# Reciprocal square roots by GpSimd's power in place of ScalarE's square root and VectorE's reciprocal

## The chip, the cores and the metric

The kernel runs on one core of a Trainium2 chip, in one launch. A core has five engines that run at the same time and wait for each other by semaphores: TensorE (PE in the profile; its weight loads are PEld), VectorE (DVE), ScalarE (ACT), GpSimd (POOL) and SyncE (SP, which only issues DMAs here). The metric is the device time of one execution, in microseconds (us). The time before is the median of three executions.

## The reference

The reference is a transformer of four blocks with three layers each: a cross-attention to a long context, a mixer over the tokens themselves, and a feed-forward layer. `x` is 2 x 128 x 256 (batch, tokens, width), the context 2 x 2048 x 256, all in float32. Every layer is `x = x + layer(_layernorm(x))`. What matters here is where reciprocal square roots stand in it:

```python
def _layernorm(x, axis=-1, eps=1e-05):
    m = jnp.mean(x, axis=axis, keepdims=True)
    v = jnp.var(x, axis=axis, keepdims=True)
    return (x - m) / jnp.sqrt(v + eps)

# block 1, feed-forward (soft mixture of experts)
def _l2norm(v, axis):
    n = jnp.sqrt(jnp.sum(v * v, axis=axis, keepdims=True))
    return v / jnp.maximum(n, L2_EPS)          # L2_EPS = 1e-12; of the tokens, and of the slots mu

# block 3, cross-attention: 16 query heads, 4 key heads of 128
def _rms_norm(x, w):
    v = jnp.mean(jnp.square(x.astype(jnp.float32)), axis=-1, keepdims=True)
    return (w * (x.astype(jnp.float32) * jax.lax.rsqrt(v + EPS))).astype(x.dtype)

# block 3, mixer (a state-space layer): 64 heads, state of N = 128
def rmsnorm(x, w):
    return x * jax.lax.rsqrt(jnp.mean(x * x, axis=-1, keepdims=True) + EPS) * w
Bm = rmsnorm((x @ WB.T).reshape(B_, L, H, N), Bn_w) + B_bias
Cm = rmsnorm((x @ WC.T).reshape(B_, L, H, N), Cn_w) + C_bias
Bm = rope(Bm, theta_cumsum)
Cm = rope(Cm, theta_cumsum)
```

In block 0 the mixer's output has a gated RMS norm too. In block 3 the cross-attention normalises and rotates 2048 + 128 keys for each of the 4 key heads and the 16 query heads; the mixer's state update is computed as products of `Cm` and `Bm` between all pairs of tokens, weighted by decays.

## The kernel before, in words

Tokens lie on the 128 partitions: `x` is one tile of 128 x 2 x 256. The layers run one after another; DMAs of weights and work that hangs only on the context (keys, values, slots) are put ahead of their layer, into gaps. A scheduler places the instructions of each engine by their dependencies and priorities, except where a helper, `InOrder` (L227 in the profile, for whatever is recorded through it), keeps those of an engine in the order of the program. In the last cross-attention's main loop and in the last mixer, TensorE, VectorE and ScalarE are kept in order in this way, GpSimd is not. SBUF and PSUM buffers come from pools, and a writer waits for the last reader of the buffer.

**Norms.** `rstd` (L148) makes the reciprocal square root of a column: ScalarE's `Sqrt` with the epsilon as bias, then VectorE's `reciprocal`. `norm_rows` (L153) is a layer norm of 128 rows: `bn_stats` and `bn_aggr` give mean and variance (tile `mv`), `rstd` the factor (tile `rs`, 128 x 1), and a `tensor_scalar` the normalised rows `xn`. Most layers call it for the two batches at their start. ScalarE evaluates its functions from tables, of which it holds one set at a time; changing from `Exp` or `Sin` to `Sqrt` puts an instruction `ACT_TABLE_LOAD` into its queue, wherever its order says so. The slots' norms (class `Slots`) use a square root on ScalarE of their own.

**The last cross-attention (L3_xattn).** Eight groups, one for each key head and batch, each with 17 tiles of keys and 4 of queries (128 x 128 each). `projected` makes them by TensorE, `squared` squares them on ScalarE, `summed` reduces on VectorE to `rs` (128 x 21, in a part of 8 and one of 13 columns), `rooted` takes the square root on ScalarE, and `rotated` starts with VectorE's reciprocal and multiplies `kq` by `rs`, then by the weights, and rotates. `turn` transposes the result. While one group is prepared, the scores, the softmax (`Exp` on ScalarE into `S`), the transposes of `S` (copied by ScalarE to `pT`) and the product with the values (`py`) of the group before are worked off. The parts of the two groups alternate in an order written by hand.

**The last mixer (L3_attn).** 16 rounds: 8 groups of 8 heads, for both batches. The rounds are pipelined: in loop pass `n` the kernel works on parts of rounds `n + 1` (angles) down to `n - 3` (gate). In a pass, for its own round, TensorE projects `pb` (`projected`; Bm and Cm of 8 heads, 128 x 1024 each), ScalarE squares them into `bc`, VectorE reduces (`squares`) to `rs` (128 x 16), and `rooted` and `scaled` follow. `scaled` is VectorE's reciprocal and 16 multiplications by ScalarE, `bc<-pb,rs`. VectorE's `decay_inputs` (`lm<-tri_incl,la`) and the last step of the angles (`sc<-mm,sc`) stand behind it. In the next pass `biased` multiplies `bc` by the norm's weights and adds the biases, `rotated` turns it into `ro`, and `turned` transposes it into `rT` by TensorE with copies by ScalarE. Then `products` and `decayed` (VectorE's `m<-mm,ex`, and GpSimd's `affine_select` of it), and `mixed` on TensorE (`mm<-m,xb`). `inputs` are GpSimd's two multiplications `xb<-xp,u` and `xb<-xp,cs`, into one buffer for each batch, which they may write when the `mixed` that read it two rounds before has ended. Since the norm's `Sqrt` and the angles' `Sin` are in different table sets, an activation of one column, `warm`, calls `Sqrt` ahead of the copies of `turned`, so that its table is loaded there:

```python
            if now:
                act.activation(warm, g.eps6, AF.Sqrt)
            if rot and n - 1 < last:
                rot.turned()
            if now:
                now.squares(0)
                now.squares(1)
                now.rooted()
            ...
            if now:
                now.scaled(halves if n == last else (slice(0, HG),))
            if nxt:
                nxt.decay_inputs()
            ...
            if mix and n - 2 < last:
                mix.mixed()
```

Of the kernel before, what the change touches and what calls it, by code (L numbers as in the profile page):

```python
# [12 lines left out]
F32 = mybir.dt.float32  # L13
# [4 lines left out]
AF = mybir.ActivationFunctionType  # L18
ALU = mybir.AluOpType
# [3 lines left out]
P = 128  # L23
B = 2
D = 256
# [10 lines left out]
class Net:  # L36


    def __init__(self, ctx, tc, ins):
        self.tc = tc  # L40
        self.nc = nc = tc.nc
        self.ins = ins
        self.n_copy = 0
        self.const = ctx.enter_context(tc.tile_pool(name="const", bufs=1, reuse_waits="tile"))
        self.small = ctx.enter_context(tc.tile_pool(name="small", bufs=2, reuse_waits="tile"))
        self.act = ctx.enter_context(tc.tile_pool(name="act", bufs=1, reuse_waits="tile"))

        c = self.const
        self.x = c.tile([P, B, D], F32, name="x")
        for b in range(B):  # L50
            nc.scalar.dma_start(self.x[:, b, :], ins["x"][b])

        self.ident = c.tile([P, P], F32, name="ident")
        make_identity(nc, self.ident)
        self.identb = c.tile([P, P], BF16, name="identb")
        make_identity(nc, self.identb)
        self.ones = c.tile([P, P], F32, name="ones")
        nc.vector.memset(self.ones, 1.0)

        self.tri_incl = c.tile([P, P], F32, name="tri_incl")  # L60
        nc.gpsimd.affine_select(out=self.tri_incl, in_=self.ones, pattern=[[1, P]],
                                compare_op=ALU.is_ge, fill=0.0, base=0, channel_multiplier=-1)

        self.tri_lt = c.tile([P, P], F32, name="tri_lt")
        nc.gpsimd.affine_select(out=self.tri_lt, in_=self.ones, pattern=[[1, P]],
                                compare_op=ALU.is_ge, fill=0.0, base=-1, channel_multiplier=-1)
        self.tri_gt = c.tile([P, P], F32, name="tri_gt")
        nc.gpsimd.affine_select(out=self.tri_gt, in_=self.ones, pattern=[[-1, P]],
                                compare_op=ALU.is_ge, fill=0.0, base=-1, channel_multiplier=1)

        self.causal = c.tile([P, P], F32, name="causal")
        nc.vector.memset(self.causal, 0.0)
        nc.gpsimd.affine_select(out=self.causal, in_=self.causal, pattern=[[-1, P]],
                                compare_op=ALU.is_ge, fill=-1e30, base=0, channel_multiplier=1)

        self.bd16 = c.tile([P, P], F32, name="bd16")
        self.blocks(self.bd16.rearrange("p (k j) -> p k j", j=16), self.ones.rearrange("p (k j) -> p k j", j=16), P // 16)
        self.iota16 = c.tile([P, 16], F32, name="iota16")
        iota_i = c.tile([P, 16], I32, name="iota_i")
        nc.gpsimd.iota(iota_i, pattern=[[1, 16]], base=0, channel_multiplier=0)  # L80
        nc.vector.tensor_copy(self.iota16, iota_i)
        self.eps5 = c.tile([P, 1], F32, name="eps5")
        nc.vector.memset(self.eps5, 1e-5)
        self.eps6 = c.tile([P, 1], F32, name="eps6")
        nc.vector.memset(self.eps6, 1e-6)
        self.half_pi = c.tile([P, 1], F32, name="half_pi")
        nc.vector.memset(self.half_pi, math.pi / 2)

# [56 lines left out]
        else:  # L145
            self.nc.vector.tensor_copy(out, in_)

    def rstd(self, out, in_, scale, eps, act=None):  # L148
        nc = self.nc
        (act or nc.scalar).activation(out, in_, AF.Sqrt, bias=eps, scale=scale)  # L150
        nc.vector.reciprocal(out, out)

    def norm_rows(self, out, in_, act=None):  # L153

        nc = self.nc
        st = self.sm([P, 6], "st")
        nc.vector.bn_stats(st, in_)
        mv = self.sm([P, 2], "mv")
        nc.vector.bn_aggr(mv, st)
        rs = self.sm([P, 1], "rs")  # L160
        self.rstd(rs, mv[:, 1:2], 1.0, self.eps5, act)
        nc.vector.tensor_scalar(out, in_, mv[:, 0:1], rs, ALU.subtract, ALU.mult)

    def layernorm(self):
# [185 lines left out]
class Values:  # L350


    KVH, HD = 4, 128
# [344 lines left out]
def l0_attn(g):  # L698

    nc, tc = g.nc, g.tc  # L700
# [4 lines left out]
    with tc.tile_pool(name="l0a", bufs=2, reuse_waits="tile") as p:  # L705
# [6 lines left out]
        act = InOrder(tc, nc.scalar)  # L712
# [26 lines left out]
        for b in range(B):  # L739
            tok = slice(b * P, (b + 1) * P)  # L740
            pss = g.mm([P, 1])
            g.project(pss, lambda c: osq[:, c, tok], lambda c: g.ones[:, 0:1])
            rs = g.sm([P, 1], "rs")
            g.rstd(rs, pss, 1.0 / D, g.eps5)
            po = g.mm([P, D])
            g.project(po, lambda c: yT[:, c, tok], lambda c: wo[:, c, :])
            nc.vector.scalar_tensor_tensor(g.x[:, b, :], po, rs, g.x[:, b, :], ALU.mult, ALU.add)
# [124 lines left out]
def l1_mixing(g, ctxT):  # L872


    nc, tc = g.nc, g.tc
# [3 lines left out]
    with tc.tile_pool(name="l1x", bufs=2, reuse_waits="tile") as p:  # L879
        mix, dd = g.mixing, g.mixing.dd  # L880
        act = InOrder(tc, nc.scalar)

        def normed(b, n):
            xn = p.tile([P, D], F32, tag="xn", name="xn")
            g.norm_rows(xn, g.x[:, b, :], act)
            if n:
                g.values.step(n)
            else:
                g.busy(8)
            ps = g.tr([P, 2, P])  # L890
            for c in range(2):
                nc.tensor.transpose(ps[:, c, :], xn[:, c * P:(c + 1) * P], g.ident)
            o = p.tile([P, 2, P], F32, tag="xT", name="xT")
            g.copy(o, ps)
            return o
# [92 lines left out]
def l1_ffn(g, mu, b1):  # L988
# [4 lines left out]
    nc, tc = g.nc, g.tc  # L993
    E, SL, H = 16, 128, 64
    with tc.tile_pool(name="l1f", bufs=2, reuse_waits="tile") as p:
# [13 lines left out]

        ee = p.tile([P, 1], F32, name="ee", bufs=1)
        nc.vector.memset(ee, 1e-10)
        xl = p.tile([P, B, D], F32, name="xl", bufs=1)
        xu = p.tile([P, B, D], F32, name="xu", bufs=1)
        g.values.step(2)
        for b in range(B):
            st = g.sm([P, 6], "st")
            nc.vector.bn_stats(st, g.x[:, b, :])
            mv = g.sm([P, 2], "mv")  # L1020
            nc.vector.bn_aggr(mv, st)
            rs = g.sm([P, 1], "rs")
            g.rstd(rs, mv[:, 1:2], 1.0 + 1e-5, ee)
            nc.vector.scalar_tensor_tensor(xl[:, b, :], g.x[:, b, :], mv[:, 0:1], gam, ALU.subtract, ALU.mult)
            nc.vector.scalar_tensor_tensor(xl[:, b, :], xl[:, b, :], rs, bet, ALU.mult, ALU.add)
            n2 = g.sm([P, 1], "n2")
            nc.scalar.activation(xu[:, b, :], xl[:, b, :], AF.Square, accum_out=n2)
            nc.scalar.activation(n2, n2, AF.Sqrt)
            nc.vector.tensor_scalar(n2, n2, 1e-12, None, ALU.max)
            nc.vector.reciprocal(n2, n2)  # L1030
            nc.vector.tensor_scalar(xu[:, b, :], xl[:, b, :], n2, sc, ALU.mult, ALU.mult)
        xlT = g.transposed(xl, "oT")
        for b in range(B):
# [396 lines left out]
def l3_xattn(g, ctxT, cos, sin, values):  # L1430
# [6 lines left out]
    nc, tc = g.nc, g.tc  # L1437
    KVH, REP, HD = 4, 4, 128
# [3 lines left out]
    pe, dve, act, pp = nc.tensor, nc.vector, nc.scalar, None  # L1442
    with ExitStack() as ctx:
# [18 lines left out]
        class Group:  # L1462
# [47 lines left out]
                dve.tensor_reduce(self.rs[:, lo:hi], self.rot[:, lo:hi, :], AX.X, ALU.add)  # L1510

            def rooted(self, lo, hi):
                act.activation(self.rs[:, lo:hi], self.rs[:, lo:hi], AF.Sqrt, bias=g.eps6, scale=1.0 / HD)

            def rotated(self, lo, hi):

                kq, rot, b = self.kq, self.rot, self.b
                n = hi - lo
                dve.reciprocal(self.rs[:, lo:hi], self.rs[:, lo:hi])
                dve.tensor_tensor(kq[:, lo:hi, :], kq[:, lo:hi, :], self.rs[:, lo:hi].unsqueeze(2).to_broadcast([P, n, HD]), ALU.mult)  # L1520
                parts = []
                for k0, k1, w in ((lo, min(hi, KT), kw), (max(lo, KT), hi, qw)):
# [3 lines left out]
                    if k0 < KT:  # L1526
                        c, s = cos[:, b, k0:k1, :], sin[:, b, k0:k1, :]
                    else:
                        c, s = (u[:, b, NT, :].unsqueeze(1).to_broadcast([P, k1 - k0, 64]) for u in (cos, sin))
# [79 lines left out]
        xn = g.act.tile([P, B, D], F32, tag="xn", name="xn")  # L1609
# [9 lines left out]
        now = Group(*todo[0])  # L1619
# [41 lines left out]
        for n in range(len(todo)):  # L1661
# [46 lines left out]
            now = nxt  # L1708
# [3 lines left out]
def l3_attn(g):  # L1712


    nc, tc = g.nc, g.tc
    H, HG, N = 64, 8, 128
    TURN = 6.283185
    with tc.tile_pool(name="l3w", bufs=2, reuse_waits="tile") as pw, tc.tile_pool(name="l3a", bufs=1, reuse_waits="tile") as p, tc.tile_pool(name="l3t", bufs=2, reuse_waits="tile") as p2, \
# [107 lines left out]
        class Round:  # L1826
# [65 lines left out]
                dve.tensor_reduce(self.rs[:, a * HG:(a + 1) * HG], self.bc[:, a], AX.X, ALU.add)  # L1892

            def rooted(self):
                act.activation(self.rs, self.rs, AF.Sqrt, bias=g.eps6, scale=1.0 / N)

            def scaled(self, parts=(slice(0, HG),)):
                dve.reciprocal(self.rs, self.rs)
                for hs in parts:
                    for a in range(2):  # L1900
                        for i in range(hs.start, hs.stop):
                            act.mul(self.bc[:, a, i, :], self.pbs[a][:, i, :], self.rs[:, a * HG + i:a * HG + i + 1])
# [65 lines left out]
        todo = [(hg, b) for hg in range(H // HG) for b in range(B)]  # L1968
        last = len(todo) - 1
        halves = (slice(0, HG // 2), slice(HG // 2, HG))  # L1970
        warm = g.sm([P, 1], "warm")
        rounds = {n: Round(*todo[n]) for n in range(2)}

        first, second = rounds[0], rounds[1]
# [26 lines left out]
        for n in range(1, len(todo) + 3):  # L2001
# [44 lines left out]
                    pass  # L2046
            if nxt:
                nxt.summed_angles()
            if now:
                act.activation(warm, g.eps6, AF.Sqrt)  # L2050
            if rot and n - 1 < last:
                rot.turned()
            if now:
# [316 lines left out]
```

## Time and profile before

| | |
|---|---|
| executions | 1536.5, 1530.4, 1533.33 us; median 1533.33 |
| profiled execution | 1536.08 us, span 1534.3 us |
| mean granted clock of TensorE | 0.921 of full speed |
| busy: PE, DVE, ACT, POOL | 1411.2, 1125.0, 810.0, 148.0 us |
| L3_xattn, about 735 to 1100 us | 7 groups of some 53 us behind the first |
| L3_attn, about 1140 to 1480 us | 16 rounds, 19.67 us apart in the steady part |

All times in the profile are us from the start of the span unless marked ns. A group of instructions is written as line, engine, operation and `out<-in` with the names of the tiles (buffer numbers left out), then the shapes and the count. Idle time in front of an instruction stands in brackets with what ended it. Spans on POOL are rough, and the ends of matmuls are modelled.

### The profile page before, as it was taken

To read this page: it belongs to the slowest core of one execution; us is meant where nothing else is said; L and a number is where in the kernel's file an instruction comes from. 1 tells how busy PE (TensorE), PEld (TensorE's weight loads), DVE (VectorE), ACT (ScalarE), POOL (GpSimd) and SP (SyncE) were. 2 spreads that over 40 slices of the span, in tenths; PEclk is the share of its full clock that TensorE was granted. 3 is DMA by queue.
4 is the path that set the end of the run, shared out by engine and by line. 5 is a ranking of instruction groups with operands and counts; after the bars stand their busy time and mean duration, and the time that the engine had idled before them with its cause. 6 is when DMAs were issued, how large, how long until landed. Compare 5 with 4: busy or idle time off the path is not lost.

```text
span 1534.3 us, 18452 instructions
## 1 busy us (share of the span) xinstructions
PE 1411.2 (92%) x6936; PEld 877.6 (57%) x6936; DVE 1125.0 (73%) x1970; ACT 810.0 (53%) x1251; POOL 148.0 (10%) x140
## 2 busy tenths in 40 slices
PE   7849997899889999989999999999888999999978
PEld 5513333667456786655656656665544666666667
DVE  6889997576356476675776776777547999999976
ACT  3567776323333433454554455455447888877711
POOL 6720001002000000000000000000000211111100
PEclk9955555899999999999999999999999999999999
DMA  6799999744350342312001000000152222221110
GB/s 186 140 174 202 206 202 199 227 151 132 97 159 22 102 136 62 121 44 66 29 0 55 29 26 16 28 28 1 35 218 83 78 88 97 96 97 42 35 35 7
DMA packets 225139, 143.87 MB, mean 94 GB/s; under 512 B 177897, under 2 KB 203769, under 8 KB 220698
## 3 DMA queue, kind: packets, MB, share of 16 engines
q1 hardware_dynamic: 221696, 140.75, 35.2%
q10 hardware_dynamic: 3290, 1.77, 0.4%
q8 instruction: 55, 0.90, 0.2%
q0 software_dynamic: 64, 0.18, 0.1%
q14 instruction: 34, 0.28, 0.1%
HBM read 90.33 MB, written 8.65 MB: 65 GB/s over the span
## 4 chain that ended last, share of the span: by engine, by line
PE 66%; DVE 19%; ACT 7%; DMA 3%; issue 2%; POOL 2%; ACTq 0%; SPq 0%; DVEq 0%; POOLq 0%
PE mm L227 13%; PE wide L227 9%; PE mm L184 8%; DVE S L227 8%; PE py L227 8%; PE pb L227 6%; PE tr L227 5%; PE acc L1235 2%; DMA pT<-Si 2%; PE acc L227 2%; PE sc L227 1%; PE one L227 1%; DVE bc L227 1%; POOL kn L227 1%; ACT L227 1%
## 5 line engine op out<-in xcount | busy, mean ns | idle before, releaser
L227 DVE TENSOR_SCALAR_CACHE_REDUCE S<-sc 128x1024 f32<-128x1024 f32 x128 | 150.5, 1219 | 6.9 <-PE sc L227 3.4
L227 PE MATMUL py<-pT,v 128*128 128x512 f32 x272 | 141.1, 605 | 9.5 <-ACT pT L227 9.5
L227 PE MATMUL sc<-kT,qT 48*128 48x512 bf16 x256 | 130.0, 614 | 20.8 <-DMA kT<-kpad 6.5
L227 ACT ACTIVATE Si<-S,nb,sq 128x4096 int16<-128x4096 f32 (+1 forms) x35 | 122.7, 3507 | 42.9 <-issue 27.8
L227 ACT COPY pT<-tr 128x512 f32<-128x512 f32 x136 | 78.7, 584 | 82.8 <-PE tr L227 82.8
L227 PE MATMUL wide<-kT,qT 128*128 128x512 f32 x256 | 116.6, 598 | 0.0
L227 ACT ACTIVATE S<-S,nb 128x2176 f32<-128x2176 f32 x32 | 67.5, 2108 | 92.5 <-DVE nb L227 92.5
L227 PE MATMUL pb<-wb,xT 128*128 128x512 f32 x256 | 112.5, 592 | 0.0
L227 PEld LDWEIGHTS tr<-ident,S 128*128 128x128 f32 x544 | 67.5, 141 | 68.4 <-issue 37.7
L227 DVE TENSOR_SCALAR_CACHE_REDUCE S<-wide 128x1024 f32<-128x1024 f32 x64 | 77.7, 1223 | 27.8 <-PE wide L227 27.4
L227 ACT ACT_TABLE_LOAD x72 | 92.4, 1283 | 5.0 <-PE mm L227 3.0
L227 PEld LDWEIGHTS <-pT 128*128 128x128 bf16 x1024 | 36.4, 105 | 94.7 <-issue 87.0
L227 PE MATMUL tr<-ident,S 128*128 128x128 f32 x544 | 81.4, 274 | 3.5 <-ACT S L227 3.3
L227 PEld LDWEIGHTS pb<-wb,xT 128*128 128x128 f32 x256 | 48.8, 191 | 59.8 <-issue 56.0
L227 PEld LDWEIGHTS wide<-kT,qT 128*128 128x128 f32 x256 | 47.5, 193 | 50.3 <-issue 43.5
L227 ACT ACTIVATE bc<-pb,rs 128x128 f32<-128x128 f32 x256 | 68.0, 435 | 0.9 <-DVE rs L227 0.9
L227 ACT ACTIVATE bc<-pb 128x1024 f32<-128x1024 f32 x32 | 32.8, 1024 | 63.5 <-PE pb L227 63.5
L227 PE MATMUL mm<-m,xb 128*64 128x128 f32 x512 | 60.2, 275 | 2.9 <-DVE m L227 1.9
L227 PEld LDWEIGHTS mm<-m,xb 128*64 128x64 f32 x512 | 55.4, 137 | 6.7 <-DVE m L227 2.6
L184 PE MATMUL mm<-wvs,ctxT 128*128 128x512 f32 x116 | 57.0, 614 | 0.0
L227 PE MATMUL wide<-w,ctxT 128*128 128x128 f32 x448 | 53.0, 277 | 2.6 <-DVE S L227 2.6
L227 PE MATMUL mm<-xT,w 128*128 128x256 f32 x216 | 55.3, 404 | 0.0
(540 smaller groups left out, 2874.4 us busy)
## 6 DMA issues: line engine op xcount, KB each, us to landing
w<-in_L_ffn_w_dram SPq DMA_DIRECT2D x25, 384.0 KB
vs<-st SPq DMA_DIRECT2D x32, 256.0 KB
v<-vs SPq DMA_DIRECT2D x8, 1024.0 KB
wb<-in_L_attn_WB_dram SPq DMA_DIRECT2D x8, 1024.0 KB
wb<-in_L_attn_WC_dram SPq DMA_DIRECT2D x8, 1024.0 KB
bb<-in_L_attn_BC_bias_dram SPq DMA_DIRECT2D x8, 1024.0 KB
ctxT<-in_ctxT_dram SPq DMA_DIRECT2D x15, 512.0 KB
w<-in_ctx_dram SPq DMA_DIRECT2D x8, 512.0 KB
```

The source lines that it names most:

```text
L184: self.nc.tensor.matmul(out, lhsT=lhsT(c), rhs=w(c), start=(c == 0), stop=(c == n - 1))
L227: return lambda *a, **k: self.tc.keep_in_program_order(f(*a, **k))
L1235: nc.tensor.matmul(acc[c], lhsT=kf[:, i, c * P:(c + 1) * P], rhs=cx[:, t % 4 + i, :], start=(t + i == 0), stop=(t + i == NT - 1))
```

## The change

`rstd` no longer uses ScalarE or VectorE's reciprocal. VectorE's `tensor_scalar` multiplies by the scale and adds the epsilon, and GpSimd's `tensor_tensor` raises the result to the power -0.5, which stands in a constant tile of 32 columns, `power`. The norms of L3_xattn, of L3_attn and of the tokens in block 1's feed-forward layer are changed alike, and the activation `warm` is removed. The slots' norms stay. The core of the diff:

```diff
-        self.eps5 = c.tile([P, 1], F32, name="eps5")
-        nc.vector.memset(self.eps5, 1e-5)
-        self.eps6 = c.tile([P, 1], F32, name="eps6")
-        nc.vector.memset(self.eps6, 1e-6)
+        self.power = c.tile([P, 32], F32, name="power")
+        nc.vector.memset(self.power, -0.5)
...
-    def rstd(self, out, in_, scale, eps, act=None):
+    def rstd(self, out, in_, scale, eps):
         nc = self.nc
-        (act or nc.scalar).activation(out, in_, AF.Sqrt, bias=eps, scale=scale)
-        nc.vector.reciprocal(out, out)
+        nc.vector.tensor_scalar(out, in_, scale, eps, ALU.mult, ALU.add)
+        nc.gpsimd.tensor_tensor(out, out, self.power[:, 0:1], ALU.pow)
...
             n2 = g.sm([P, 1], "n2")
             nc.scalar.activation(xu[:, b, :], xl[:, b, :], AF.Square, accum_out=n2)
-            nc.scalar.activation(n2, n2, AF.Sqrt)
-            nc.vector.tensor_scalar(n2, n2, 1e-12, None, ALU.max)
-            nc.vector.reciprocal(n2, n2)
+            nc.vector.tensor_scalar(n2, n2, 1e-24, None, ALU.max)
+            nc.gpsimd.tensor_tensor(n2, n2, g.power[:, 0:1], ALU.pow)
...
             def rooted(self, lo, hi):                       # L3_xattn
-                act.activation(self.rs[:, lo:hi], self.rs[:, lo:hi], AF.Sqrt, bias=g.eps6, scale=1.0 / HD)
+                dve.tensor_scalar(self.rs[:, lo:hi], self.rs[:, lo:hi], 1.0 / HD, 1e-6, ALU.mult, ALU.add)
+                nc.gpsimd.tensor_tensor(self.rs[:, lo:hi], self.rs[:, lo:hi], g.power[:, lo:hi], ALU.pow)
...
             def rotated(self, lo, hi):
...
-                dve.reciprocal(self.rs[:, lo:hi], self.rs[:, lo:hi])
...
             def rooted(self):                               # L3_attn
-                act.activation(self.rs, self.rs, AF.Sqrt, bias=g.eps6, scale=1.0 / N)
+                dve.tensor_scalar(self.rs, self.rs, 1.0 / N, 1e-6, ALU.mult, ALU.add)
+                nc.gpsimd.tensor_tensor(self.rs, self.rs, g.power[:, 0:2 * HG], ALU.pow)
 
             def scaled(self, parts=(slice(0, HG),)):
-                dve.reciprocal(self.rs, self.rs)
...
-        warm = g.sm([P, 1], "warm")
...
-            if now:
-                act.activation(warm, g.eps6, AF.Sqrt)
```

More of the change, by code (lines that the diff above doesn't have):

```diff
@@ L146, in copy, with norm_rows @@
             self.nc.vector.tensor_copy(out, in_)
-    def rstd(self, out, in_, scale, eps, act=None):
+    def rstd(self, out, in_, scale, eps):
         nc = self.nc
-        (act or nc.scalar).activation(out, in_, AF.Sqrt, bias=eps, scale=scale)
-        nc.vector.reciprocal(out, out)
-    def norm_rows(self, out, in_, act=None):
+        nc.vector.tensor_scalar(out, in_, scale, eps, ALU.mult, ALU.add)
+        nc.gpsimd.tensor_tensor(out, out, self.power[:, 0:1], ALU.pow)
+    def norm_rows(self, out, in_):
         nc = self.nc
@@ L160, in norm_rows @@
         rs = self.sm([P, 1], "rs")
-        self.rstd(rs, mv[:, 1:2], 1.0, self.eps5, act)
+        self.rstd(rs, mv[:, 1:2], 1.0, 1e-5)
         nc.vector.tensor_scalar(out, in_, mv[:, 0:1], rs, ALU.subtract, ALU.mult)
@@ L743, in l0_attn @@
             rs = g.sm([P, 1], "rs")
-            g.rstd(rs, pss, 1.0 / D, g.eps5)
+            g.rstd(rs, pss, 1.0 / D, 1e-5)
             po = g.mm([P, D])
@@ L884, in normed @@
             xn = p.tile([P, D], F32, tag="xn", name="xn")
-            g.norm_rows(xn, g.x[:, b, :], act)
+            g.norm_rows(xn, g.x[:, b, :])
             if n:
@@ L1008, in l1_ffn @@
         nc.gpsimd.memset(xw[:, :, :, H:H + 1], 1.0)
-        ee = p.tile([P, 1], F32, name="ee", bufs=1)
-        nc.vector.memset(ee, 1e-10)
         xl = p.tile([P, B, D], F32, name="xl", bufs=1)
@@ L1022, in l1_ffn @@
             rs = g.sm([P, 1], "rs")
-            g.rstd(rs, mv[:, 1:2], 1.0 + 1e-5, ee)
+            g.rstd(rs, mv[:, 1:2], 1.0 + 1e-5, 1e-10)
             nc.vector.scalar_tensor_tensor(xl[:, b, :], g.x[:, b, :], mv[:, 0:1], gam, ALU.subtract, ALU.mult)
```

## The prediction

> **What bounds the kernel now.** I read the page's busy line and chain first, then busy time by stage, then the timeline of one round of the stage that looked closest to its limit, and last the rows of the tile `rs`, which every norm writes.
>
> ```profile
> PE 1411.2 (92%) x6936; PEld 877.6 (57%) x6936; DVE 1125.0 (73%) x1970; ACT 810.0 (53%) x1251; POOL 148.0 (10%) x140
> ...
> PE 66%; DVE 19%; ACT 7%; DMA 3%; issue 2%; POOL 2%; ACTq 0%; SPq 0%; DVEq 0%; POOLq 0%
> ```
>
> TensorE carries the end, and only 7% of the chain, some 107 us, is ScalarE. So the ScalarE time removed (sum below) can't come back whole. Busy time by stage (columns: stretch, length, then busy us and instructions of PE, PEld, DVE, ACT, POOL, then granted clock):
>
> ```profile
> 735.00:1100.00 365.00, 349.85 (x1624) 218.56 (x1624) 269.67 (x502) 182.05 (x255) 1.06 (x1) 1.00 0.08 26
> 1140.00:1480.00 340.00, 321.65 (x1499) 199.60 (x1498) 299.91 (x325) 255.33 (x533) 57.57 (x66) 0.99 0.22 82
> 1222.60:1242.28 19.68, 19.58 (x94) 12.11 (x93) 18.28 (x20) 15.70 (x34) 3.65 (x4) 1.00 0.21 80
> ```
>
> The first is the last block's cross-attention (L3_xattn), the second its 16-round mixer (L3_attn), the third one mixer round. In a round TensorE and VectorE are both nearly full: whatever lengthens a chain between VectorE instructions there lengthens the round. One round's norm, VectorE, then ScalarE, then GpSimd (start, length, instruction, in brackets the idle time before it):
>
> ```profile
> 1254.30 2.33 DVE L227 TENSOR_REDUCE rs<-bc 128x8 f32<-128x1024 f32 x2
> 1257.01 0.25 DVE L227 RECIPROCAL rs<-rs 128x16 f32<-128x16 f32 x1 [0.38 <-ACT rs L227]
> 1257.18 1.16 DVE L227 TENSOR_TENSOR lm<-tri_incl,la 128x1024 f32<-128x1024 f32 x1
> 1258.26 0.68 DVE L227 TENSOR_TENSOR sc<-mm,sc 128x512 f32<-128x512 f32 x1
> 1259.55 1.29 DVE L227 TENSOR_TENSOR bc<-bc,nw 128x1024 f32<-128x1024 f32 x1 [0.62 <-ACT bc L227]
> ```
>
> ```profile
> 1253.29 1.28 ACT L227 ACT_TABLE_LOAD   x1
> ...
> 1256.67 0.31 ACT L227 ACTIVATE rs<-rs,eps 128x16 f32<-128x16 f32 x1
> ...
> 1257.35 3.46 ACT L227 ACTIVATE bc<-pb,rs 128x128 f32<-128x128 f32 x13
> ```
>
> ```profile
> 1251.05 1.49 POOL L1952 TENSOR_SCALAR_AFFINE_SELECT m<-m 128x512 f32<-128x512 f32 x1 [9.72 <-DVE m L227]
> 1254.45 0.63 POOL L1952 TENSOR_SCALAR_AFFINE_SELECT m<-m 128x512 f32<-128x512 f32 x1 [1.91 <-DVE m L227]
> 1259.47 0.29 POOL L1941 TENSOR_TENSOR xb<-xp,u 128x64 f32<-128x64 f32 x1 [4.38 <-PE mm L227]
> 1259.72 1.28 POOL L1941 TENSOR_TENSOR xb<-xp,cs 128x64 f32<-128x64 f32 x1
> ```
>
> Call the end of the reduction R (1256.63). The root, the reciprocal and the first eight of the `bc` multiplications take until R + 2.92, where VectorE's own `bc` multiplication (`biased`) begins after 0.62 us of idling. From there VectorE runs 16.74 us nearly without a gap to the next R: 2.92 + 16.74 = 19.66, the round's period. So R to `biased` is on the path in every round. The table load of the round (1253.29) lies before R and is hidden, with `warm` behind it.
>
> **What goes.** 55 of 101 table loads: 55 x 1.283 = 70.6 us of ScalarE, with the 61 small square roots, of 0.20 to 0.31 us each. Where was such a load on the path?
>
> In each of the seven later L3_xattn groups, the load stands between the softmax's exponential and the copy of `pT` that TensorE waits for:
>
> ```profile
> 786.21 1.28 ACT L227 ACT_TABLE_LOAD   x1
> 787.51 0.30 ACT L227 ACTIVATE rs<-rs,eps 128x8 f32<-128x8 f32 x1
> 787.71 1.05 ACT L227 COPY pT<-tr 128x512 f32<-128x512 f32 x2
> ...
> 788.33 1.12 PE L227 MATMUL py<-pT,v 128*128 128x512 f32 x2 [1.32 <-ACT pT L227]
> ```
>
> Without load and root the copy starts when TensorE has two transposes of `tr` done (about 786.65): 1.06 us a group, 7 x 1.06 = 7.4 us. The load back to Exp was hidden (ScalarE waits 3.5 us for VectorE there). At ScalarE's load the Trainium skill ("ScalarE: Activation LUTs", What ACT_TABLE_LOAD costs) adds a drain of some 1.38 us to the 1.28 us of the load; in this trace the root starts 0.02 us behind the load, so no such drain shows. By the page the groups would give about 7 x 2.4 = 17 us, by the row 7.4.
>
> Single places: at the start a load (12.06 to 13.34) delays the first norm, about 1 us; at 529.03 another, 1.3 us; around 645.8 and 676.0 two that TensorE waits for, 2 us taken (0 to 4, as the scheduler also reorders this stretch). Sum of the gains: 7.4 + 1 + 1.3 + 2 = 11.7 us. The other loads ran ahead of their norm and cost nothing.
>
> **What is added.** The rows of `rs` (count; least, median and most ns; first and last start):
>
> ```profile
> L227 DVE RECIPROCAL rs<-rs x30: 202/248/254, 734.5 to 1453.6; 128x16 f32<-128x16 f32 x16, 128x8 f32<-128x8 f32 x7, 128x13 f32<-128x13 f32 x7
> L151 DVE RECIPROCAL rs<-rs x26: 130/164/165, 13.7 to 1482.8; 128x1 f32<-128x1 f32 x26
> ```
>
> 61 powers on GpSimd (one for each reciprocal: these 30 + 26, three more of `rs` around 660 and two of `n`) and as many small tensor_scalars on VectorE (128x1 takes 0.15 us, 0.15 to 0.2 at 128x16) where the reciprocals were (0.16 and 0.25): VectorE's sum stays. No row shows a power. Below it stand multiplications of 128x64 at 0.29 alone, above them 128x1024 at 1.93; a single column is a memset of 0.10 at the least. I take the geometric middles: X16 = 0.75 (0.29 to 1.93), X1 = 0.44 (0.10 to 1.93).
>
> *The norms of 128x1.* From the aggregate's end to `xn` the chain is 0.56 (at 1130.05 to 1130.61); after it is 0.15 + two handovers of 0.06 + X1. Each gains or loses X1 - 0.3, some eleven of them on the path: 11 x 0.14, about +1.5 us (-2 to +18). Behind the `tensor_scalar` that makes `xn` VectorE's queue waits as it did for the reciprocal, and TensorE's transposes wait for `xn`. GpSimd's other work delays none: at the start its memsets end at 12.1, and the expansion's DMA, now queued behind a power at 278, is needed only near 305. SP's queue is shifted a little and idles anyway.
>
> *L3_xattn's powers* (128x8, 128x13) lie in VectorE's chain, which idled 0.46 and 1.05 for the root; the chain has some 1.9 us to spare at the group's end: nothing, up to 2.9 us each.
>
> *The mixer.* Before, the reciprocal held VectorE until R + 0.55, and `lm` (two inputs in SBUF) followed. Now VectorE has only the tensor_scalar, then starts `lm` at R + 0.16, just as GpSimd gets the power. The trace speaks on this: the affine select of 1.49 us starts beside a rotation of VectorE (`ro`, two SBUF inputs) and ends 0.5 us behind it, the one beside nothing takes 0.63; `xb<-xp,cs` takes 1.28 beside `bc<-bc,nw`, and 0.30 at 1479.42 alone. So GpSimd is held until VectorE is done: the power ends at R + 0.16 + 1.16 - 0.1 + X16 = R + 1.22 + X16; ScalarE then needs 0.05 and eight multiplications (2.2), `biased` starts at R + 3.47 + X16, against 2.92: 0.55 + X16 = 1.30 us a round. The Trainium skill ("SBUF — State Buffer", Who interferes with whom) says the same of a VectorE instruction with two SBUF inputs against a GpSimd instruction that reads SBUF, as a lock for the whole instruction, and so speaks against the change.
>
> Should the power start ahead of `lm` all the same, it would end at R + 0.22 + X16 and `biased` begin at R + 2.47 + X16: a round would cost X16 - 0.45.
>
> GpSimd's calls are placed by the scheduler, not by the hand-written order. In the changed kernel's order, as built, six of the sixteen powers (those of rounds 4, 5, 8, 9, 12 and 13, counted from 0) stand behind the `xb` pair, which waits for the end of TensorE's `mixed` (R + 2.84, first row 1259.47). There the two `xb` multiplications end at R + 3.35, the power at R + 3.4 + X16, and `biased` begins at R + 5.65 + X16: 2.75 + X16 more than now. But `mixed` can itself move up: without load and `warm`, ScalarE's copies `rT`, which free the buffers of the transposes ahead of `mixed`, come up to 1.5 us earlier, and a longer round gives TensorE room; then the affine select (1254.45 + 0.63 = R - 1.55) is its limit, 1.1 us earlier or so. Between 1.65 + X16 and 2.75 + X16 I take the middle, 2.2 + X16 = 2.95 us a round. Queued behind the waiting `xb` is just that power, and behind it ScalarE's 16 multiplications, VectorE's `bc` and the transposes.
>
> Round 0 is in the run-in, where no engine is full, and is left out. Sum for the mixer: 9 x 1.30 + 6 x 2.95 = 29.4 us (least: X16 at 0.29 with 1.65, 7.6 + 11.6 = 19; most: 1.93 with 2.75, 22.3 + 28.1 = 50). ScalarE's round shrinks by 1.28 + 0.20 + 0.31, but it wasn't the bound.
>
> **The sum.** The profiled execution took 1536.08 us (span 1534.3). 1536.1 - 11.7 + 1.5 + 29.4 = 1555.3, a change of +19.2; on the median of 1533.33 that is 1552.5, and I forecast 1553.
>
> **Rivals.**
> 1. *Loads win* (faster). The power starts ahead of `lm`, and the order of the `xb` pair doesn't matter because `mixed` has ended by R in those rounds. Then the mixer costs 15 x (X16 - 0.45), between -2 and +5 with X16 up to 0.75, and the gains stand: 1533.3 - 11.7 + 1.5 + 0 = about 1523. For it: the load is visibly on TensorE's path in L3_xattn. Against: the starting times of `lm` and `mixed`. It decides if the mixer's norm costs below 0.7 us a round.
> 2. *A dear power* (slower still). X16 at 1.93 and X1 at 1: mixer 46 to 50, norms 11 x 0.7 = 8, gains 11.7: 1533 + 45 = 1578. For it: no row prices the function, a power is more than a multiplication. It decides from X16 = 1.5.
> 3. *No change*: `mixed` has ended by R + 0.7, so that only the port holds, in all 15 rounds, with X16 = 0.3: 15 x 0.85 = 12.8 against 11.7, and the norms at nothing: 1534.
>
> **How the numbers follow.** My case 0.53 (19 to 40 us in the mixer: 1542 to 1563), the dear power 0.14, no change 0.13, loads win 0.20. Runs of this kernel spread 0.4%, so about 0.5%, 7.7 us, is what can be told from none. Faster 0.20, same 0.13, slower 0.67. The range leaves out the tails of the rivals on both sides: 1522 to 1580.
>
> **What would show it.** Right: the mixer's period at about 21.0 us in nine rounds and 22.6 in six, `xb` ahead of the power in the latter, GpSimd's power ending with `lm`, VectorE idle before `bc<-bc,nw` at 2 to 4 us; L3_xattn shorter by 7 us with `pT` right behind the exponential. Wrong: a period of 19.7 or less in the mixer, a power under 0.3 us or over 2 us, or drains that vanish along with the loads (L3_xattn shorter by over 12 us).

## The result, and the profile after

The changed kernel takes 1589.92 us (median of four runs, 1588.18 to 1590.79) against 1532.95 (the three executions of above and a fourth): a ratio of 1.0361, 95% interval 1.0339 to 1.0383. It is slower by 57 us, where 20 were forecast, and outside the stated range. The profiled execution has a span of 1587.3 us, 53.0 more than before.

Busy time and the chain that ended last, from the page:

```profile
PE 1427.5 (90%) x6936; PEld 882.7 (56%) x6936; DVE 1118.3 (70%) x1966; ACT 724.5 (46%) x1120; POOL 236.2 (15%) x201
...
PE 56%; DVE 26%; POOL 6%; ACT 5%; issue 4%; DMA 2%; POOLq 0%; DVEq 0%; ACTq 0%
```

ScalarE lost some 85 us of work, and the chain went from TensorE (66% before) to VectorE and GpSimd. The mixer's 16 rounds show where. One round of each of two kinds, by the table of stretches (columns as before):

```profile
1287.50:1310.13 22.63, 19.68 (x94) 12.01 (x93) 18.03 (x20) 14.13 (x30) 6.37 (x5) 1.00 0.27 100
1357.84:1382.92 25.08, 19.68 (x94) 12.01 (x93) 18.32 (x20) 14.13 (x30) 5.53 (x5) 1.00 0.23 76
```

The work of TensorE and VectorE is the same as in the 19.67 us round of before; 3 and 5.4 us of waiting are added. In both TensorE was granted its full clock (1.00), so a lower clock isn't what lengthens them. The norm in a round of the first kind, VectorE, then ScalarE, then GpSimd:

```profile
1312.35 0.17 DVE L225 TENSOR_SCALAR rs<-rs 128x16 f32<-128x16 f32 x1
1312.43 1.22 DVE L225 TENSOR_TENSOR lm<-tri_incl,la 128x1024 f32<-128x1024 f32 x1
1313.57 0.68 DVE L225 TENSOR_TENSOR sc<-mm,sc 128x512 f32<-128x512 f32 x1
1318.64 1.23 DVE L225 TENSOR_TENSOR bc<-bc,nw 128x1024 f32<-128x1024 f32 x1 [4.39 <-ACT bc L225]
```

```profile
1316.44 3.46 ACT L225 ACTIVATE bc<-pb,rs 128x128 f32<-128x128 f32 x13 [3.63 <-POOL rs L1891]
```

```profile
1312.67 3.74 POOL L1891 TENSOR_TENSOR rs<-rs,power 128x16 f32<-128x16 f32 x1 [1.91 <-DVE rs L225]
1316.38 0.29 POOL L1936 TENSOR_TENSOR xb<-xp,u 128x64 f32<-128x64 f32 x1
```

And GpSimd in a round of the second kind, where the reduction ended at R = 1360.02:

```profile
1362.79 0.29 POOL L1936 TENSOR_TENSOR xb<-xp,u 128x64 f32<-128x64 f32 x1 [4.31 <-PE mm L225]
1363.04 0.29 POOL L1936 TENSOR_TENSOR xb<-xp,cs 128x64 f32<-128x64 f32 x1
1363.29 2.90 POOL L1891 TENSOR_TENSOR rs<-rs,power 128x16 f32<-128x16 f32 x1
```

The picture is the forecast one, with `lm` beside the power, `xb` ahead of it in six rounds, ScalarE and VectorE waiting for it. But the power itself takes 2.90 us alone and 3.74 beside `lm`, where the sum had 0.75. By widths, from the rows of `rs` (count, form, busy time, mean ns; then idle time before):

```profile
L1509 POOL TENSOR_TENSOR rs<-rs,power 128x13 f32<-128x13 f32 x7 | 17.0, 2427 | 75.7 <-DVE rs L225 75.7
L1509 POOL TENSOR_TENSOR rs<-rs,power 128x8 f32<-128x8 f32 x9 | 14.9, 1652 | 267.7 <-DVE rs L225 247.4 <-DVE rs L1508 20.3
L149 POOL TENSOR_TENSOR rs<-rs,power 128x1 f32<-128x1 f32 x26 | 14.7, 573 | 226.2 <-DVE rs L148 226.2
```

The last cross-attention, on the other hand, gained what was forecast. Its ScalarE rows, where a table load and a root stood between the exponential and `pT`:

```profile
783.49 0.19 ACT L225 ACTIVATION_READ_ACCUMULATOR S<-S,nb 128x1 f32 x1
784.09 1.08 ACT L225 COPY pT<-tr 128x512 f32<-128x512 f32 x2 [0.42 <-PE tr L225]
```

Its groups are 52.29 us apart instead of 53.37. By places in the two traces: the mixer's first layer norm (`mv`) comes 7.5 us earlier (1122.37 against 1129.87), from there to the norm behind the mixer it takes 409.9 us instead of 350.3 (+59.6), and what follows 0.9 more: -7.5 + 59.6 + 0.9 = +53.0, the difference of the spans. The first of the three is known to a few us only: in three kernels that are alike up to the mixer (the one before, and two of the experiments below, mixer only and price) this norm comes at 1129.87, 1133.09 and 1128.26. The second repeats: 409.1 in the mixer-only kernel, and 350.6 to 353.3 in the others that keep the old mixer.

### The profile page after: what moved, and what is told of

Same layout as the page of the kernel before. It is cut to its first block, busy times and chain, and to the rows that moved or that the text cites. A ratio compares the mean times of both kernels' runs of the same rounds, so it can differ in the third digit from the quotient of the medians.

```text
span 1587.3 us, 18423 instructions
## 1 busy us (share of the span) xinstructions
PE 1427.5 (90%) x6936; PEld 882.7 (56%) x6936; DVE 1118.3 (70%) x1966; ACT 724.5 (46%) x1120; POOL 236.2 (15%) x201
## 4 chain that ended last, share of the span: by engine, by line
PE 56%; DVE 26%; POOL 6%; ACT 5%; issue 4%; DMA 2%; POOLq 0%; DVEq 0%; ACTq 0%
PE wide L225 10%; PE mm L182 8%; PE mm L225 7%; PE py L225 7%; DVE S L225 6%; PE tr L225 4%; DVE bc L225 4%; DVE ro L225 4%; POOL rs L1891 3%; PE sc L225 3%; ACT bc L225 2%; PE pb L225 2%; DVE rs L225 2%; PE acc L1230 2%; PE acc L225 2%
## 5 line engine op out<-in xcount | busy, mean ns | idle before, releaser
L225 PE MATMUL sc<-kT,qT 48*128 48x512 bf16 x256 | 130.2, 615 | 19.5 <-DMA kT<-kpad 6.5
L225 PE MATMUL pb<-wb,xT 128*128 128x512 f32 x256 | 121.7, 631 | 26.6 <-ACT bc L225 26.6
L225 DVE TENSOR_TENSOR bc<-bc,nw 128x1024 f32<-128x1024 f32 (+1 forms) x34 | 39.3, 1157 | 77.7 <-ACT bc L225 77.5
L1509 POOL TENSOR_TENSOR rs<-rs,power 128x8 f32<-128x8 f32 (+2 forms) x17 | 33.4, 1965 | 355.8 <-DVE rs L225 323.1
L1947 POOL TENSOR_SCALAR_AFFINE_SELECT m<-m 128x512 f32<-128x512 f32 x32 | 33.1, 1036 | 224.3 <-DVE m L225 224.3
L225 ACT COPY rT<-mm 128x512 f32<-128x512 f32 x64 | 33.5, 599 | 53.5 <-PE mm L225 53.4
L1891 POOL TENSOR_TENSOR rs<-rs,power 128x16 f32<-128x16 f32 x16 | 52.9, 3304 | 33.2 <-DVE rs L225 31.0
```

The costliest lines, as they stand in the source:

```text
L225: return lambda *a, **k: self.tc.keep_in_program_order(f(*a, **k))
L1509: nc.gpsimd.tensor_tensor(self.rs[:, lo:hi], self.rs[:, lo:hi], g.power[:, lo:hi], ALU.pow)
L1891: nc.gpsimd.tensor_tensor(self.rs, self.rs, g.power[:, 0:2 * HG], ALU.pow)
L1947: nc.gpsimd.affine_select(out=self.m2[:, ns, :], in_=self.m1[:, ns, :], pattern=[[0, 4], [1, P]], compare_op=ALU.is_ge, fill=0.0, base=-1, ...
```

## The experiments

Theory: the whole loss is in the mixer, and there it is made of the power's own length (2.90 us), the held port (0.83 us in nine rounds) and the place behind `xb` (about 2.5 us in six). Rivals: the loss is spread over all norms; the way by GpSimd and its queue costs that much whatever the operation; or the queue's order alone does it.

**Which norms lose.** Four kernels share out the change.

The power in the last cross-attention only:

```diff
 before.py, L3_xattn
-  act.activation(self.rs[:, lo:hi], self.rs[:, lo:hi], AF.Sqrt, bias=g.eps6, scale=1.0 / HD)
+  dve.tensor_scalar(self.rs[:, lo:hi], self.rs[:, lo:hi], 1.0 / HD, 1e-6, ALU.mult, ALU.add)
+  nc.gpsimd.tensor_tensor(self.rs[:, lo:hi], self.rs[:, lo:hi], g.power[:, lo:hi], ALU.pow)
...
-  dve.reciprocal(self.rs[:, lo:hi], self.rs[:, lo:hi])
```

> The kernel before with the power only in the last cross-attention's norms. By the traces its group shortens from 53.37 to 52.29 us, seven times, so 7.6 us less than before: about 1525.5 us. If instead the powers of 1.65 and 2.43 us there ate the gain elsewhere, within 2 us of before.

1528.04 us, ratio 0.9971 (0.9956 to 0.9987). A little faster, by 4.6 us in the medians (2.0 to 6.7 by the interval), between the 7.6 expected and its rival's 2. In its trace the groups are 52.30 us apart, so the two powers of 1.65 and 2.43 us in a group are covered; why 3 us of the gain don't show in the time is open.

The power in `rstd` and the tokens' norms only (the diff's first and second part on the kernel before):

> The kernel before with the power only in the 128x1 norms (layer norms, the gated norm, the tokens' norms). With 0.55 us for a power of one column each norm on the path loses about 0.25 us, some eleven of them 2.8 us, and two table loads off the path give back about 2: 1532 to 1536 us, no difference that can be told. A rival that gives the norms a large share of the 57 us would have it above 1545.

1531.61 us, ratio 0.9999 (0.9983 to 1.0016): nothing that can be told. The 26 powers of one column are not where the time went.

The power in the mixer only (the diff's parts in L3_attn on the kernel before):

> The kernel before with the power only in the last mixer. If the whole loss is there, it is larger than that of the full change: 1533 + 59 = 1592 us. If the loss is spread over the kernel, clearly less.

1595.23 us, ratio 1.0392 (1.0359 to 1.0425), with periods of 22.6 and 25.1 us as in the changed kernel.

And the reverse, the changed kernel with the mixer's part taken back:

```diff
 after.py, L3_attn
-  dve.tensor_scalar(self.rs, self.rs, 1.0 / N, 1e-6, ALU.mult, ALU.add)
-  nc.gpsimd.tensor_tensor(self.rs, self.rs, g.power[:, 0:2 * HG], ALU.pow)
+  act.activation(self.rs, self.rs, AF.Sqrt, bias=g.eps6, scale=1.0 / N)
...
+  dve.reciprocal(self.rs, self.rs)                 # scaled()
...
+  act.activation(warm, g.eps6, AF.Sqrt)            # ahead of turned()
```

> The changed kernel with square root, reciprocal and the warm activation back in the last mixer only. If the mixer alone loses, 1533 - 7.6 and the norms' part, 1524 to 1529 us, faster than before; if the losses elsewhere are real, above 1533.

1527.36 us, ratio 0.9966 (0.9948 to 0.9984). So the loss is in the mixer and nowhere else; the rival of many small losses is out. The three parts, -4.6, -1.1 and +62.6 us, each against the kernel before as timed beside it, add up to the 57 of the whole change.

**What in the mixer loses.** First the operation, all else equal:

```diff
-  nc.gpsimd.tensor_tensor(self.rs, self.rs, g.power[:, 0:2 * HG], ALU.pow)
+  nc.gpsimd.tensor_tensor(self.rs, self.rs, g.power[:, 0:2 * HG], ALU.mult)
```

> The changed kernel with a multiplication in place of the power in the mixer's 16 GpSimd calls (same operands, same queue order; so the mixer's norm isn't computed). If the power's own 2.9 us is what the sum lacked, the mixer still pays the held port (about 0.5 to 0.8 us in nine rounds) and the place behind xb (about 2.8 us in six): 5 to 7 and 17 us, 1533 - 7 + 23 = 1549 us. If waiting for GpSimd and its queue made the loss, whatever the operation, over 1575.

1551.23 us, ratio 1.0103 (1.0053 to 1.0154). The multiplication takes 0.22 us where nothing holds it. Most rounds without `xb` in front take 19.95 us, and those with it 22.4 (two took about 24). With the power's own length 38.7 us go, and some 19 remain: 26 for the way by GpSimd in the mixer, less the 7.5 gained elsewhere.

Then the port: the other VectorE instruction first, which has one input in PSUM.

```diff
-            if nxt:
-                nxt.decay_inputs()
             for _ in reduced:
                 pass
+            if nxt:
+                nxt.decay_inputs()
```

> The changed kernel with VectorE's sc (one input in PSUM) ahead of lm (two inputs in SBUF) behind the mixer's reduction, so that the power starts with the port free. If the 3.74 us against 2.90 is a held port, the power takes 2.90 in all rounds and nine rounds give back 0.83 each: 1582 us. Rival: lm is then held by the power, the decays on TensorE come later by up to 2 us, and the time stays at 1590.

1592.35 us, ratio 1.0374 (1.0324 to 1.0425): no gain in time. Yet the trace shows the part that was asked for. GpSimd in a round without `xb` in front:

```profile
1315.27 2.90 POOL L1891 TENSOR_TENSOR rs<-rs,power 128x16 f32<-128x16 f32 x1 [1.90 <-DVE rs L225]
```

The power takes 2.90 us instead of 3.74, and these rounds 21.80 us instead of 22.63, 0.83 less, as expected. In this run two of the rounds with `xb` in front took 26.69 us instead of 25.08, and the run-in of the mixer (from the start of round 0's reductions to that of round 1's) 37.6 us instead of 34.0. In both places TensorE worked at a lower clock. Ahead of one of the two long rounds:

```profile
1334.01 3.48 PE L225 MATMUL mm<-ident,ro 128*128 128x128 f32 x16
1337.42 3.78 PE L225 MATMUL mm<-m,xb 128*64 128x128 f32 x32
```

and in the run-in:

```profile
1152.90 8.93 PE L225 MATMUL pb<-wb,xT 128*128 128x512 f32 x16
```

The 16 transposes took 1.96 us in the changed kernel (from 1332.24); here they ran at a granted clock of 0.53 (1334.0 to 1337.4). `mixed` stands behind them, and `xb` and the power wait for it, so all came 1.5 us later; the other round of 26.69 us has transposes of 3.29 us in that place. The `pb` matmuls of the run-in took 7.03 us in the changed kernel; from 1150 to 1174 the granted clock was 0.86, against 0.97 there. Whether the shift of `lm` or chance brought the lower clock about isn't settled by this run; the rival, that the held port only moves, gets no support from the nine rounds, nor from the kernel with both changes below.

Next the place in the queue:

```diff
-        pe, dve, act = InOrder(tc, nc.tensor), InOrder(tc, nc.vector), InOrder(tc, nc.scalar)
+        pe, dve, act, pool = (InOrder(tc, e) for e in (nc.tensor, nc.vector, nc.scalar, nc.gpsimd))
...  # the power, xb and the affine select by pool instead of nc.gpsimd
```

> The changed kernel with the mixer's GpSimd calls kept in the order of the program, which puts the power ahead of the xb pair in all rounds. By the two periods (25.08 and 22.62 us) six rounds give back 2.46 each: 1589.9 - 14.8 = 1575 us. If the order had no part, 1590.

1579.85 us, ratio 1.0289 (1.0237 to 1.0341): 10 us back of the 14.8 expected. The six rounds take 23.02 instead of 25.08, 12.4 us in all; in the profiled execution 3.7 of them went in the run-in (37.6 us again instead of 34.0, with a `pb` of 8.96 us and a granted clock of 0.86). The fastest of the four runs, at 1575.14, is where the expectation was.

Both together:

> The changed kernel with both: GpSimd's calls in the mixer kept in the order of the program, and VectorE's sc ahead of lm. If place and held port add up, every round takes the 21.80 us that the unheld rounds took, against 22.63 to 23.02: 1579.9 - 15 x 1.0 = 1565 us. If taking away both waits only moves the loss, 1575 or more.

1564.22 us, ratio 1.019 (1.0165 to 1.0216), as expected. Rounds take 21.8 and 22.2 us, and the run-in 34.0 again. Place and port together are worth 26 us of the 57. In the rounds that nothing else disturbed their gains add up; the medians of the two kernels with one of them alone (10 us less, 2.4 more) do not, since those kernels had the long run-in, and one of them the long rounds too.

And both, with the multiplication:

> The same with a multiplication in place of the power in the mixer (the norm there isn't computed). If the power's length, its place and the held port are the whole of the mixer's loss, nothing is left of it: a period of 19.7 us, 1524 to 1528 us in all. If the way by GpSimd costs something besides, a period above 20 us and over 1530.

1530.63 us, ratio 0.9984 (0.9965 to 1.0003), with a period of 19.5 us. The period is that expected (below 20 us); the time is 3 us over, and just beyond the 1530 that the expectation gave to a further cost. By the trace the mixer, from its first norm to the norm behind it, takes 351.3 us against 350.3 before the change, so most of the 3 us lie elsewhere. With the power's length gone too, nothing of the mixer's loss is left in its rounds: the way by GpSimd costs them no time in itself. The three steps from 1589.9 are 10 (place), 16 (port) and 34 us (length) in this order; taken first, the port gave nothing and the length 38.7.

**The price of the power.**

```diff
+        for n in (1, 2, 4, 8, 16, 32, 64):
+            for op in (ALU.pow, ALU.mult):
+                for _ in range(2):
+                    pool.tensor_tensor(o[:, 0:n], v[:, 0:n], pw[:, 0:n], op)
+        # and powers of 1 and 16 columns on 32 and 64 partitions
```

> The kernel before with GpSimd instructions behind its end: power and multiplication of 128 x 1, 2, 4, 8, 16, 32 and 64, each twice, and powers on 32 and 64 partitions. From 0.55, 1.65, 2.43 and 2.90 us at 1, 8, 13 and 16 columns the power takes 0.39 + 0.157 us for each column: 5.4 at 32 and 10.4 at 64, where the multiplication stays below 0.30. Rival: a fixed start of over 1 us that wide powers spread. The partitions should make no difference.

Single powers and one with half the partitions, from the groups of that kernel in narrow windows (form, count, busy time, mean ns of one):

```profile
L227 POOL TENSOR_TENSOR bo<-bv,bw 128x16 f32<-128x16 f32 x1 | 2.9, 2899 | 0.1
...
L227 POOL TENSOR_TENSOR bo<-bv,bw 128x32 f32<-128x32 f32 x1 | 5.4, 5426 | 0.1
...
L227 POOL TENSOR_TENSOR bo<-bv,bw 128x64 f32<-128x64 f32 x1 | 10.5, 10545 | 0.1
...
L227 POOL TENSOR_TENSOR bo<-bv,bw 64x16 f32<-64x16 f32 x1 | 2.9, 2906 | 0.1
```

From 16 to 64 columns that is (10.545 - 2.899) / 48 = 0.159 us a column, from 1 to 16 (2.90 - 0.55) / 15 = 0.157, on top of 0.39; the partitions don't matter. A multiplication of 64 columns takes 0.29 (`xb` above), a power 10.5.

**A version with the gain and without the loss.** The mixer's power in halves, each behind its own reduction, in kept order:

```diff
                 now.squares(0)
+                now.rooted(0)
                 now.squares(1)
-                now.rooted()
+                now.rooted(1)
...  # rooted(a): tensor_scalar and pool's power on the 8 columns of a
```

> As the kernel with the kept order, and the mixer's power in two halves of eight columns, the first right behind its half of the reduction. It starts 1.0 us ahead of the reduction's end R and takes 1.65, so ScalarE's first eight multiplications can start at about R + 0.7 as before the change: a period of 19.7 to 20 us, and 1525 to 1530 us in all. If ScalarE waits for both halves, the period is about 22.3 and the time near 1568.

1526.99 us, ratio 0.996 (0.9937 to 0.9982): 62.9 us less than the changed kernel, with as many columns of power. VectorE and GpSimd in a round:

```profile
1320.23 1.21 DVE L225 TENSOR_REDUCE rs<-bc 128x8 f32<-128x1024 f32 x1
1321.48 0.17 DVE L225 TENSOR_SCALAR rs<-rs 128x8 f32<-128x8 f32 x1
...
1325.67 1.27 DVE L225 TENSOR_TENSOR bc<-bc,nw 128x1024 f32<-128x1024 f32 x1 [0.97 <-ACT bc L225]
```

```profile
1321.80 3.80 POOL L225 TENSOR_TENSOR rs<-rs,power 128x8 f32<-128x8 f32 x2 [0.78 <-DVE rs L225]
```

The first power runs beside a reduction, and ScalarE can begin with it; the second, held by `lm` in part, ends 2.8 us behind the reductions while ScalarE still works on the first half. VectorE idles 0.97 us instead of 4.39, and the periods are 19.5 and 19.8 us. Halves without the kept order were not run.

The same, with the norms of 128x1 left on ScalarE and VectorE:

> The power in the last cross-attention and, in halves and in kept order, in the last mixer; the 128x1 norms stay on ScalarE and VectorE. The cross-attention gives 7.6 us, the mixer's halves nothing (TensorE is full at 19.7 us a round), the norms nothing: 1525 to 1528 us, faster than both kernels. Rival: the sum of single gains goes on, below 1522.

1526.43 us, ratio 0.9944 (0.9926 to 0.9962). It beats both kernels, but is not to be told from the two versions above (1526.99 and 1527.36). In all three traces the cross-attention's groups are 52.3 us apart and the mixer takes 350.6 to 351.5 us, no less than the 350.3 of before: it is the cross-attention that gains.

## Why the prediction was right or wrong

**The step that failed is X16**, the price of a power of 16 columns: 0.75 us in the sum, 1.93 as its upper bound, 2.90 measured. I had placed it between two multiplications by their numbers of elements. A row of another operation bounds neither the time for an element nor the start: the power's 0.157 us a column is some ninety times what the multiplications cost at the margin ((1933 - 290) / 960 = 1.7 ns a column, by the rows I used). In 15 rounds the miss is 15 x 2.15 = 32 us, and the forecast was 37 too low. Single columns (0.55, not 0.44) add 1.2, and 4 are the footing of the sum: it was built on a profiled execution, and the two of these lie 53.0 us apart, the medians 57.0. A power of over 2 us was among the prediction's own signs of being wrong.

With 2.90 in place of 0.75, and 0.55 for a single column, the prediction's own sum gives 9 x 3.45 + 6 x 5.10 = 61.7 us for the mixer, where the trace shows 59.6. So the mechanism held and its size was off. That the two are so near is in part luck: by the paragraphs below, the sum has 0.5 us too much in each of the nine rounds and 0.3 too little in each of the six, and round 0, which it left out, took 1.8 us more (32.24 against 30.40 from its reductions' end to round 1's).

**The held port** was right. The power beside `lm` ends at R + 4.10 (1316.41, with R at 1312.31), where R + 1.22 + 2.90 = R + 4.12 was the formula; without `lm` it takes 0.83 us less. The Trainium skill's rule ("SBUF — State Buffer", Who interferes with whom), that such a VectorE instruction contends with GpSimd's reads, agrees with both.

**The place behind `xb`** was right in its six rounds, but the hope that `mixed` would move up was not: `xb` started at R + 2.77, as before at R + 2.84. TensorE's transposes ahead of `mixed` start 0.14 us behind the end of VectorE's last `ro` in both kernels (1357.32 behind 1357.18, before 1253.93 behind 1253.79), and take 1.96 us, against 2.03 to 2.19: that 0.1 to 0.2 us is all that earlier copies could give. Without that hope the sum would lose 2.75 + 2.90 = 5.65 in such a round; 5.4 was measured.

**The round's other part** was a little shorter than the sum's. From `biased` to the next R VectorE takes 16.3 us instead of 16.74, so nine rounds lost 2.96 and not 3.45.

**The gains.** L3_xattn: 1.08 us a group against 1.06. The drain of 1.38 us behind a table load, which the Trainium skill states ("ScalarE: Activation LUTs", What ACT_TABLE_LOAD costs), would have made it 2.4; the groups show none. Of the single places, the one at 529.03 gave what was forecast: from the aggregate to `xn` it takes 1.02 us (530.53 to 531.55) instead of 2.22 (528.63 to 530.85), though the layer itself came 1.9 us later in this execution. At the start no gain can be told: `xn` comes at 12.65 us instead of 13.88, but at 11.94 in the mixer-only kernel, which keeps the load. The 128x1 norms by themselves gave nothing in time, so the 4.3 us taken for these places aren't seen, small beside the rest.

**The rivals.** The dear power was the right one of them, and its price (1578) too low for the same reason: both of its ends were multiplications. "Loads win" needed a power ahead of `lm` and `mixed` over by R, neither of which happened; "no change" needed `mixed` over by R + 0.7 and a cheap power, and `mixed` let `xb` go at R + 2.77.

## What to carry to other kernels

An operation that no row shows is not bounded by rows of other operations, however many elements they have; a forecast that multiplies it by 15 rounds should say so in its range. What a slow instruction costs is decided by its place: the same 16 columns of power a round cost 59 us in one piece behind the last reduction and next to nothing in halves and in kept order, the first of them a reduction earlier. Where some queues are kept in order and one is not, its order has to be read from the built kernel, since a single waiting instruction put in front cost 2.5 us a round.

## What the runs showed of the hardware

GpSimd's power of -0.5 takes 0.39 us and 0.157 us for each column, whatever the number of partitions (32 to 128), against 0.22 us for a multiplication of 16 columns.

GpSimd was held by a VectorE instruction with two inputs in SBUF: the same power took 3.74 us beside `lm` and 2.90 with `lm` moved away.

TensorE's granted clock was lower behind some of its waits. In the changed kernel's mixer the 16 matmuls of `pb` took 7.13 us behind each of seven waits of 0.8 to 1.1 us. Behind six waits of 3.2 us they took 8.83, 10.17, 8.68, 7.13, 8.76 and 7.13; the granted clock was 0.70 over the 10.17 us (from 1272.11; that round lasted 26.0 us) and 1.00 over those from 1368.45. In the kernel with `sc` ahead of `lm` a wait of 1.81 us and two matmuls came before the transposes at 0.53; behind the same wait at 1311.08 they ran at their usual length. What decides it isn't shown.
